# Four graph-attention layers: other all-node row tiles in layer 2, and other pools for the gathered rows

## The chip, the cores and the metric

The kernel runs on one core of a Trainium2 chip. The time is device time in microseconds, taken over several executions; beside it stands one execution recorded by the hardware profiler, with every instruction of the engines: PE (TensorE, matmuls; PEld are its weight loads), DVE (VectorE), ACT (ScalarE), POOL (GpSimd) and SP (SyncE, which issues most DMAs). Lower is better.

## The reference

There are 4096 nodes with 256 features and an adjacency matrix that has about 17 ones in a row of 4096 (each entry is one with probability 0.0039, and the diagonal is set). Four layers follow each other; each computes attention over the neighbours, adds it to its input and normalizes the row:

```python
# layers 0 and 1: 4 heads of 64; layer 2: 2 heads of 128; layer 3: 1 head, on x with both signs
e = leaky_relu(s1[:, None] + s2[None, :], 0.2)        # s1, s2: projections of x
att = softmax(where(adj > 0, e, -big), axis=1)
h = att @ Wh                                          # layer 3: also -softmax(-e) @ x, then fc_W and elu
x = layernorm(x + h)
```

Each layer needs the whole result of the layer before: a node's neighbours may lie anywhere.

## The kernel before

The 4096 rows are 32 row tiles of 128. The kernel keeps a table of projected rows in DRAM for each layer (the features times their exponentials, and the score terms), and works on a row tile in one of two ways.

A **sparse row tile** (class `RowTile`) collects only rows that its 128 nodes need. Lists made once from the adjacency (in layer 0, `lists`) name them. They are split in two parts. The *first part* (`half` 0) is the tile's own 128 rows, loaded by SP (line 808), and six indirect gathers of 128 rows each by GpSimd (line 813); these six read only rows of row tiles 0 to 22 (`MIX` is 23). The *second part* (`half` 1) is seven gathers that may read any row. So the first parts of a layer can be gathered once tiles 0 to 22 of the layer before are projected, and second parts only when all are. ACT then computes exponentials from the gathered score terms (line 923 in layers 0 to 2, 890 to 893 in layer 3), DVE masks them (925, 892, 894), and PE multiplies (946), 14 matmuls for a part and 28 instructions in the profile, since a float32 matmul is two.

An **all-node row tile** gathers nothing. `WHOLE` (line 115) lists, by layer, groups of up to four neighbouring row tiles that are computed densely against all 32 tiles of nodes: a pass of 32 units, each with one load of projected rows (`vw`, line 1206), the exponentials on ACT (1218; in layer 3, 1221 to 1225), the mask on DVE (1219, 1226) and matmuls for each tile of the group (1229). Layer 3 makes two passes over each group. The units are strewn between the parts of the sparse tiles by a budget (`whole`, line 1013), and all are used up some six parts before the layer's end. In layer 2, with 21 sparse and 11 all-node tiles, the passes are over 12-15, 28-31 and 25-27, in this order; the sparse tiles are 0-11 and 16-24.

**The end of a row tile.** `finish` and `norm` (lines 1395, 1339) divide, add, take the variance and scale. Several tiles share one inverse square root on DVE; `GROUPS` (line 82) says how many, by the layer and by the tile's number. Once scaled, a tile is *ready*; it is then projected for the next layer (class `Projection`: transpose on PE, copy `xT` on ACT, matmul at line 707, `row` on DVE, a store by SP at line 744), one or two per part, tiles below 23 first.

**The change of layer** (`close`, line 1124): the next layer's loads for its first row tiles are issued, ten all-node units of the next layer run ahead (`AHEAD`), the last tile is finished and projected, and the first parts of the next layer's tiles 0 and 1 are computed, in layer 3 not before the last projection.

**Slots.** Gathered rows stand in two pools of four slots, `g0` and `g1`. Up to layer 2 a part fills one slot; in layer 3, with longer rows, two. First parts use `g0`, second parts `g1`:

```python
    def slot(self, half, s):
        L, n = self.layer, self.layer.n
        if (half, s) not in self.slots:
            pool = L.prog.g1 if half else L.prog.g0
            self.slots[half, s] = pool.tile([P, SLOT], F32, name="G")
        return self.slots[half, s]
```

A slot is given out again in the order of the program; a gather or own-row load into it waits until the matmuls of its former owner are done. A planner orders the instructions of each engine before the program is built; each engine's queue, GpSimd's and SP's too, then runs strictly in that order, so that one waiting gather holds those behind it. In GpSimd's order, layer 2 begins with the first parts of tiles 0 to 3, one gather of tile 4's first part, the second parts of tiles 0 to 3, and the rest of tile 4; layer 3 begins with the first parts of tiles 0 and 1, then tile 2's and tile 3's mixed with the second parts of tiles 0 and 1.

Of the kernel before, what the change touches and what calls it, by code (L numbers as in the profile page):

```python
# [78 lines left out]
UNITS = (1 + FIRST, NPACK - FIRST)  # L79
FULL = ((0,), tuple(range(NPAIR - FIRST, NPACK - FIRST)))  # L80
PAIRS = (tuple(range(1, 1 + FIRST)), tuple(range(NPAIR - FIRST)))
GROUPS = (((24, 4),), ((24, 2), (29, 1), (31, 2)), ((16, 2), (17, 1), (20, 2), (25, 1), (31, 2)), ((25, 1), (28, 3), (31, 4)))
LEAD = 4
LATE = 4
MIX = 23
# [29 lines left out]
WHOLE = (  # L115
    (),
    (range(5, 8), range(29, 32),),
    (range(12, 16), range(28, 32), range(25, 28),),
    (range(28, 32), range(25, 28),),
)  # L120
AHEAD = 10
# [56 lines left out]
class Turns:  # L178
# [5 lines left out]
    def tile(self, *args, **kw):  # L184
        self.pools.append(self.pools.pop(0))
        return self.pools[-1].tile(*args, **kw)
# [586 lines left out]
class RowTile:  # L773
# [8 lines left out]
    def slot(self, half, s):  # L782
        L, n = self.layer, self.layer.n
        if (half, s) not in self.slots:
            pool = L.prog.g1 if half else L.prog.g0
            self.slots[half, s] = pool.tile([P, SLOT], F32, name="G")
        return self.slots[half, s]

# [8 lines left out]
    def load(self, half):  # L797
        L, m, n = self.layer, self.m, self.layer.n
        prog, nc, sh = L.prog, L.nc, L.shared
        copies = sh["v"][n]  # L800
        self.values = copies[m // BT % len(copies)]
        if half == 0:
            self.S = prog.ld.tile([P, H4, P], F32, name="S")
            nc.sync.dma_start(out=self.S[:, :TERMS[n]], in_=sh["e"][n][m].partition_broadcast(P))
            self.bits = prog.ld.tile([P, 2 * HALF, MW], I32, name="bits")
            if n > 0:
                nc.sync.dma_start(out=self.bits, in_=sh["bitsC"][m])
            nc.sync.dma_start(out=self.row(0, 0), in_=self.values[m * P:(m + 1) * P, :ROW[n]])
        else:
            self.y = L.load_x(m)  # L810
        for k in range(1 - half, HALF):
            pos = half * HALF + k - 1
            nc.gpsimd.indirect_dma_start(  # L813
                out=self.row(half, k), out_offset=None, in_=self.values[:N + 1 if half else MIX * P, :].rearrange("r (k c) -> (r k) c", k=STRIDE),
                in_offset=bass.IndirectOffsetOnAxis(ap=sh["idx"][:, m, pos:pos + 1], axis=0))
# [157 lines left out]
class Layer:  # L973
# [22 lines left out]
    def tile(self, m):  # L996
        if m not in self.tiles:
            self.tiles[m] = RowTile(self, m, self.order[m])
        return self.tiles[m]

    def load(self, m, half):
        if m < self.count and (m, half) not in self.loaded:
# [336 lines left out]
    def norm(self, y, m):  # L1339
# [8 lines left out]
        self.group.append((y, m))  # L1348
        if len(self.group) < next((size for end, size in GROUPS[self.n] if m < end), 1):
            return  # L1350
# [529 lines left out]
```

## Time and profile before

| | us |
|---|---|
| median of 3 runs (range) | 1991.31 (1989.16 to 1992.06) |
| profiled execution, its own time | 1986.33 |
| its span, first to last instruction | 1984.6 |
| PE busy | 1774.5 (89%) |
| PE weight loads busy | 1477.9 (74%) |
| ACT busy | 1560.2 (79%) |
| DVE busy | 1547.2 (78%) |
| GpSimd busy | 1386.2 (70%) |

The mean granted clock of PE is 0.939. Busy time is an average over stages with different limits; what bounds one stage is seen in windows of it. A row of a timeline gives the start, the length, the instruction and, in brackets, how long its engine was idle ahead of it and what ended that. A row of waits gives the sum, the number and the longest. DMA issue counts as idle time of the issuing engine: the 0.3 us ahead of each gather is such time. A releaser is inferred; where the one named had long been done, it was another.

### The profile page before, as it was taken

What the parts mean: (1) busy time and instruction counts of PE and PEld (TensorE: products, weight loads), DVE (VectorE), ACT (ScalarE), POOL (GpSimd) and SP (SyncE); (2) the same over time, 40 slices, a digit from 0 to 9 for tenths busy, and PEclk for the clock granted to TensorE, in tenths of its full rate; (3) what the DMA queues carried; (4) which work ended last, traced back from release to release, by engine and by line L of the source; (5) the groups of instructions that cost most, each with busy time, mean ns of one, the idle gap of its engine ahead of it and who ended that gap; (6) DMA issues with size and microseconds to landing.
All of it is one profiled execution on the core that took longest, in us unless ns stands there. A gap on an engine that the chain in (4) does not pass through costs nothing.

```text
span 1984.6 us, 47611 instructions
## 1 busy us (share of the span) xinstructions
PE 1774.5 (89%) x15397; PEld 1477.9 (74%) x15397; DVE 1547.2 (78%) x5213; ACT 1560.2 (79%) x4964; POOL 1386.2 (70%) x1387
## 2 busy tenths in 40 slices
PE   4758999999999889999999989799888999999894
PEld 3536777777777779989998779788776777777672
DVE  3457998888888788998998879688875577777765
ACT  4649989998879589999889879788783787777763
POOL 0057777777777777777777577777764777777773
PEclk8758899999999989999999999899999999999997
DMA  8799999999867767777777557677765888899883
GB/s 293 234 320 329 320 295 289 297 299 285 232 176 232 211 171 197 206 206 216 208 204 207 161 146 201 185 208 209 198 184 173 244 270 269 269 288 288 269 262 111
DMA packets 302523, 464.41 MB, mean 234 GB/s; under 512 B 91314, under 2 KB 216087, under 8 KB 302264
## 3 DMA queue, kind: packets, MB, share of 16 engines
q0 software_dynamic: 75296, 229.44, 39.9%
q1 hardware_dynamic: 222350, 227.63, 37.3%
q10 hardware_dynamic: 4618, 4.20, 0.6%
q8 instruction: 124, 2.03, 0.4%
q14 instruction: 135, 1.11, 0.2%
HBM read 412.03 MB, written 49.08 MB: 232 GB/s over the span
## 4 chain that ended last, share of the span: by engine, by line
PE 52%; DMA 13%; POOL 10%; ACT 9%; DVE 7%; issue 6%; SPq 1%; POOLq 0%; ACTq 0%; DVEq 0%
PE bank L946 25%; PE bank L1229 10%; POOL G L813 10%; DMA G<-vals,idx 7%; ACT w L923 5%; PE bank L707 5%; PE bank L1298 4%; PE bank L1296 3%; DMA raw<-in_adjB_dram 2%; DVE w L880 1%; ACT mk L415 1%; DMA vals<-row 1%; DMA G<-vals 1%; PE bank L693 1%; ACT pw L1218 1%
## 5 line engine op out<-in xcount | busy, mean ns | idle before, releaser
L813 POOL DMA_INDIRECT G<-vals,idx x1352 | 1380.9, 1021 | 568.4 <-issue 346.0
L923 ACT ACTIVATE w<-S,G 128x64 f32<-128x64 f32 (+1 forms) x3388 | 902.7, 350 | 103.7 <-DMA G<-vals,idx 88.9
L946 PE MATMUL bank<-G,w 128*64 128x130 f32 (+5 forms) x9044 | 903.7, 304 | 61.8 <-DVE w L880 51.5
L946 PEld LDWEIGHTS bank<-G,w 128*64 128x64 f32 (+1 forms) x9044 | 734.4, 156 | 208.6 <-DVE w L880 68.2
L1229 PE MATMUL bank<-vw,pw 128*128 128x129 f32 (+1 forms) x2304 | 378.5, 321 | 20.8 <-DVE pw L1219 6.0
L1229 PEld LDWEIGHTS bank<-vw,pw 128*128 128x128 f32 x2304 | 335.7, 194 | 59.1 <-issue 10.9
L880 DVE SCALAR_TENSOR_TENSOR w<-w,bank 128x1024 f32<-128x1024 f32 (+1 forms) x232 | 310.5, 1344 | 27.5 <-ACT w L923 26.5
L707 PE MATMUL bank<-wext,xT 128*128 128x268 f32 (+3 forms) x640 | 188.0, 429 | 27.6 <-ACT xT L698 26.0
L890 ACT ACTIVATE w<-S,G 128x64 f32<-128x64 f32 (+1 forms) x343 | 108.7, 352 | 75.6 <-DMA G<-vals,idx 59.9
L707 PEld LDWEIGHTS bank<-wext,xT 128*128 128x128 f32 x640 | 123.9, 210 | 51.7 <-ACT xT L698 29.2
L415 ACT ACTIVATE mk<-raw 128x1024 uint8<-128x1024 int32 x128 | 129.5, 1049 | 24.8 <-DMA raw<-in_adjB_dram 24.7
L1293 DVE SCALAR_TENSOR_TENSOR pw<-Sw,cw,mw 128x384 f32<-128x384 f32 x256 | 148.9, 609 | 0.1
L1298 PE MATMUL bank<-pw,vw 128*65 128x128 f32 x768 | 143.4, 274 | 0.0
L1219 DVE SCALAR_TENSOR_TENSOR pw<-pw,mw 128x512 f32<-128x512 f32 (+1 forms) x192 | 120.8, 642 | 28.6 <-ACT pw L1218 26.8
L1218 ACT ACTIVATE pw<-Sw,d 128x512 f32<-128x512 f32 (+1 forms) x192 | 126.3, 674 | 5.1 <-PE bank L1229 5.0
L1296 PE MATMUL bank<-vw,pw 128*128 128x65 f32 x768 | 128.0, 254 | 0.0
L1226 DVE TENSOR_TENSOR pw<-pw,mw 128x512 f32<-128x512 f32 (+1 forms) x128 | 79.0, 621 | 48.2 <-ACT pw L1223 23.4
L1296 PEld LDWEIGHTS bank<-vw,pw 128*128 128x128 f32 x768 | 113.8, 191 | 3.3 <-issue 0.7
L1221 ACT ACTIVATE pw<-Sw,d 128x512 f32<-128x512 f32 (+1 forms) x128 | 82.9, 655 | 15.6 <-PE bank L1229 5.6
L676 DVE TENSOR_TENSOR mw<-bw,pat 128x96 int32<-128x96 int32 (+1 forms) x352 | 89.0, 263 | 1.6
L698 ACT COPY xT<-bank 128x256 f32<-128x256 f32 x128 | 45.9, 360 | 48.7 <-PE bank L693 29.7
L892 DVE TENSOR_TENSOR w<-w,mk 128x512 f32<-128x512 f32 (+1 forms) x49 | 37.0, 756 | 53.7 <-ACT w L891 53.5
(197 smaller groups left out, 1908.4 us busy)
## 6 DMA issues: line engine op xcount, KB each, us to landing
raw<-in_adjB_dram SPq DMA_DIRECT2D x128, 512.0 KB
G<-vals,idx POOLq DMA_INDIRECT x1352
vw<-vals SPq DMA_DIRECT2D x128, 130.0 KB
vw<-vals SPq DMA_DIRECT2D x128, 128.5 KB
S<-edge SPq DMA_DIRECT2D x58, 256.0 KB
vw<-vals SPq DMA_DIRECT2D x96, 129.0 KB
xp<-y SPq DMA_DIRECT2D x96, 128.0 KB
y<-xp SPq DMA_DIRECT2D x96, 128.0 KB
```

The source lines that it names most:

```text
L415: nc.scalar.activation(self.mk[:, 2 * q:2 * q + 2], src, AF.Copy)
L707: nc.tensor.matmul(pp[:, :c1 - c0], self.xT[:, k, :], wext[:, k, c0:c1], start=(k == 0), stop=(k == KT - 1 and brow is None))
L813: nc.gpsimd.indirect_dma_start(out=self.row(half, k), out_offset=None, in_=self.values[:N + 1 if half else MIX * P, :].rearrange("r (k c) ...
L880: return nc.vector.scalar_tensor_tensor(pair, pair, LEAST, mh2, op0=ALU.max, op1=ALU.mult)
L923: nc.scalar.activation(w[h][:, u, rows], S[:, h, rows], AF.Exp, bias=d(g, h))
L946: nc.tensor.matmul(a, w[h][:, u, rows], b, start=half == 0 and u == 0 and (n == 3 or h == turns[0][0]), stop=half == 1, skip_group_check=True)
L1218: nc.scalar.activation(p, S[:, h, :g], AF.Exp, bias=d)
L1219: nc.vector.scalar_tensor_tensor(p, p, LEAST, mj, op0=ALU.max, op1=ALU.mult)
L1229: nc.tensor.matmul(accs[it][:, c:c + Wd], p[:, it, :], v[:, c:c + Wd], start=(j == 0 and h == heads[0]), stop=(j == NT - 1), skip_group_ch ...
L1293: nc.vector.scalar_tensor_tensor(p[h], S[:, h], c[:, j, h:h + 1], mj, op0=ALU.max, op1=ALU.mult)
L1296: nc.tensor.matmul(bu[:, it * Wd:(it + 1) * Wd], p[up][:, it, :], v[:, up * Wd:(up + 1) * Wd], start=j == 0 and it == 0, **how)
L1298: nc.tensor.matmul(bf[:Wd, it * P:(it + 1) * P], v[:, flat * Wd:(flat + 1) * Wd], p[flat][:, it, :], start=j == 0 and it == 0, **how)
```

## The change

Layer 2's row tiles 20 to 23 are all-node and 25 to 27 sparse, so that layer 2 has 20 sparse and 12 all-node tiles, in three passes of four: 12-15, 20-23, 28-31. The sparse ones are 0-11, 16-19 and 24-27. In `GROUPS`, layer 1's pairs reach up to tile 27 (24 to 28 were single before), and layer 2's grouping follows its new order. And the pools: in layer 2 the first parts of tiles 0 and 1 and all second parts use `g0`, and first parts from the third sparse tile on use `g1`; in layer 3 it is the other way round.

```diff
-GROUPS = (((24, 4),), ((24, 2), (29, 1), (31, 2)), ((16, 2), (17, 1), (20, 2), (25, 1), (31, 2)), ((25, 1), (28, 3), (31, 4)))
+GROUPS = (((24, 4),), ((28, 2), (29, 1), (31, 2)), ((24, 2), (28, 1), (31, 2)), ((25, 1), (28, 3), (31, 4)))
...
-    (range(12, 16), range(28, 32), range(25, 28),),
+    (range(12, 16), range(20, 24), range(28, 32),),
...
-            pool = L.prog.g1 if half else L.prog.g0
+            pool = L.pools(self.step, half)
...
+    def pools(self, m, half):
+
+        g0, g1 = self.prog.g0, self.prog.g1
+        if self.n < 2:
+            return g1 if half else g0
+        first, then = (g0, g1) if self.n == 2 else (g1, g0)
+        return then if half == 0 and m > 1 else first
```

In the changed program GpSimd's order at the start of layer 2 is: the first parts of tiles 0 to 5, then the second parts of tiles 0 to 5, and so on; at the start of layer 3: the first parts of tiles 0 to 3, then the second parts of tiles 0 to 3. The bits of row tiles 20 to 23 are also stored for all-node use (one store more in layer 0's list stage).

## The prediction

> **What bounds the kernel now.** I read the windows of the trace stage by stage first, then GpSimd's own timeline at the two layer changes, then the waits and PE's timeline. The stages: layer 1 runs at its even pace from 752 to 1095 us; layer 2's second parts begin to be gathered at 1134; layer 2's last gather is at 1477; layer 3's first sparse matmul is at 1528.5; PE ends at 1957. In the windows the columns are the stretch, its length, busy time (and instructions) of PE, PEld, DVE, ACT, POOL, then granted clock, DMA share, GB/s.
>
> ```profile
> 752.00:1095.00 343.00, 342.52 (x3732) 314.50 (x3731) 319.14 (x1002) 315.96 (x1226) 263.51 (x261) 1.00 0.73 207
> 1134.00:1181.00 47.00, 40.07 (x364) 37.84 (x362) 35.83 (x93) 35.34 (x93) 37.92 (x30) 1.00 0.52 141
> 1181.00:1478.00 297.00, 266.49 (x2304) 244.20 (x2305) 238.99 (x853) 234.48 (x719) 230.23 (x220) 0.96 0.72 199
> 1478.00:1528.00 50.00, 38.81 (x233) 30.54 (x232) 32.43 (x156) 21.78 (x58) 12.76 (x10) 0.90 0.48 142
> 1528.00:1568.00 40.00, 35.77 (x187) 26.93 (x185) 17.29 (x48) 24.58 (x51) 30.95 (x30) 1.00 0.84 247
> 1568.00:1716.00 148.00, 147.71 (x809) 114.18 (x810) 109.72 (x389) 116.31 (x264) 111.73 (x108) 0.99 0.86 265
> 1716.00:1800.00 84.00, 80.52 (x454) 59.03 (x453) 65.58 (x272) 62.20 (x152) 64.28 (x64) 0.98 0.90 285
> 1800.00:1900.00 100.00, 92.61 (x513) 68.84 (x513) 67.62 (x265) 72.50 (x179) 77.14 (x76) 0.97 0.88 275
> 1900.00:1957.00 57.00, 51.78 (x302) 35.89 (x298) 37.05 (x141) 37.98 (x95) 42.22 (x42) 0.97 0.80 241
> ```
>
> Layer 1 leaves PE 0.5 us idle in 343; layer 2, from 1134 to 1528, leaves it 6.9 + 30.5 + 11.2 = 48.6 us; layer 3 leaves 4.2 + 0.3 + 3.5 + 7.4 + 5.2 = 20.6 us. Why layer 2 idles is in GpSimd's timeline (start, length, and in brackets the idle time before) and in the waits from 1181 to 1528 (us, times, longest):
>
> ```profile
> 1119.48 1.38 POOL L813 DMA_INDIRECT G<-vals,idx  x1 [0.30 <-issue]
> 1134.24 4.06 POOL L813 DMA_INDIRECT G<-vals,idx  x1 [13.39 <-ACT w L923]
> 1477.23 1.03 POOL L813 DMA_INDIRECT G<-vals,idx  x1 [0.30 <-issue]
> 1512.80 1.23 POOL L813 DMA_INDIRECT G<-vals,idx  x1 [34.53 <-DMA y<-xp]
> ACT w L923 <- DMA G<-vals,idx: 55.9, 55, 2.9
> PE bank L707 <- ACT xT L698: 24.5, 11, 7.0
> PE bank L748 <- DVE row L741: 9.5, 9, 1.7
> ```
>
> GpSimd gathers without a pause from 1134 to 1478 and stands still for 13.4 us before and 34.5 us after. Its "busy" 78% is saturation: 0.30 us of issue precedes every gather of about 1 us. ACT waits for gathered rows 55 times; PE's waits for xT are the next link, since the copy stands behind those exponentials in ACT's queue. So layer 2 is bound by the gathers, with PE close behind at 90%.
>
> ```profile
> L813 POOL DMA_INDIRECT G<-vals,idx x261 | 263.5, 1010 | 79.6 <-issue 68.3 <-ACT w L923 4.3 <-DMA G<-vals,idx 2.4
> L813 POOL DMA_INDIRECT G<-vals,idx x220 | 231.1, 1050 | 67.1 <-issue 57.3 <-ACT w L923 2.7 <-PE bank L1229 1.5
> 1194.96 5.53 PE L1229 MATMUL bank<-vw,pw 128*128 128x129 f32 x48
> 1200.32 2.28 PE L946 MATMUL bank<-G,w 128*128 128x129 f32 x28
> 1206.23 2.73 PE L946 MATMUL bank<-G,w 128*128 128x129 f32 x28
> 1522.64 3.81 PE L707 MATMUL bank<-wext,xT 128*128 128x256 f32 x8 [7.03 <-ACT xT L698]
> ```
>
> These are the gather groups of layer 1's and layer 2's even stages, PE's pieces of layer 2, and the last projection, held 7 us. One gather of layer 2 costs (231.1 + 67.1) / 220 = 1.355 us.
>
> **The change, step by step.**
>
> *One sparse row tile becomes all-node.* GpSimd: 13 gathers fewer, 13 x 1.355 = 17.6 us. PE: two parts fewer, 2.28 + 2.73 = 5.0 us; the third all-node pass has four tiles instead of three, so 32 x 2 more matmuls, 128 instructions by 5.53 / 48 = 0.115, or 14.7 us. Net +9.7 us on PE. Durations of ACT and DVE are those of their groups by shape between 1134 and 1480. ACT: 28 exponentials fewer (20 by 0.285, 8 by 0.367 us, 8.6 us) and 64 wider by 0.704 - 0.578 (8.1 us): nothing. DVE: 64 wider by 0.679 - 0.539, 9.0 us, less the removed tile's masks, some 4, and less three of the inverse-root chains (the new groups make 74 of 77; 15 small instructions of 0.155, 7 us in layers 1 and 2): nothing. DVE and ACT at about 90% do not hold PE up, as layer 1's row shows (93% and 92% beside a full PE). SP: one more store of 256 KB in the list stage, at most 0.9 us at that stage's 290 GB/s, at least nothing; I take nothing, since 25 us of waits for raw loads are spread over that stage. Score rows and y loads balance.
>
> *The pools at the change to layer 2.* The 25th gather of layer 2 (1134.24) waited for a slot that row tile 0's first part held until its matmuls ended at 1133.5. In the changed program's order, first parts of tiles 4 and 5 stand ahead of all second parts and take slots that layer 1 let go by 1112. So 12 gathers, not one, fill the gap: 1120.9 + 12 x 1.3 = 1136.5. Tile 0's second part starts there, as before, but GpSimd is 11 gathers ahead (15 us). Layer 1's pairs (24, 25) and (26, 27) put one more projection into its closing: up to 3 us later, or 1 earlier; I take nothing, because GpSimd is occupied until 1136 anyway.
>
> *Layer 2's body.* Gathers left at 1136: 260 - 36 = 224, so the last is near 1136 + 304 = 1440, not 1477. PE's work is then the longer: from 1181 (until then both kernels wait for four contiguous second parts) 266.5 + 38.8 + 9.7 = 315 us, to 1496. Kept idle: the row-to-transpose waits, some 8 us. Layer 3's first sparse matmul comes at 1504 instead of 1528.5: **-24**.
>
> *The change to layer 3.* The 34.5 us wait is for row tile 22's projected rows: the first-part gathers read tiles 0 to 22, and 22 was the third last sparse tile. Now 20 to 23 are done in the second pass, and the last of them is 19, projected some 35 us of PE work before layer 3's first matmul: 10 us in four parts, 20 in eight projections, 5 in all-node units. Gathers can start near 1474. Tiles 0 and 1 take the slots of layer 2's first parts, 2 and 3 those of its second parts, so none waits for layer 3. All 24 are out near 1506, and the second parts follow when the last rows are written. Before, 10 were out at 1528.5. Lead gained: 14 gathers, 19 us, less 5: tile 1's second part now needs the slot of tile 1's first part, whose matmuls stand behind 52 all-node matmuls (11.5 us). On SP, the own-row loads of tiles 2 and 3 now wait for layer 2's last second parts, with four row stores behind them; bounded by 0 and the 2.7 us of a part, taken as nothing: the last projection comes later anyway.
>
> *Layer 3's body.* 1568 to 1716 is full and stays. Of the 20.6 us idle, a load of vw (3.0), the z copy between passes (5.3), a reciprocal (2.5) and vw again (2.1) are no gathers; the 8 left go, as the 14 us lead is larger: **-8**.
>
> *Clock.* The granted clock was 0.96 and 0.90 in layer 2's body and tail and 1.00 in the full stage. That is 297 x 0.04 + 50 x 0.10 = 17 us of clock lost, between none and most of it in working time; I take 4: **-4**.
>
> Sum: -24 - 8 - 4 = -36 us. The profiled execution took 1986.3; 1950 follows for its like. The median, 1991.3, lies 5.0 above it, so **1955** for the median.
>
> **Rules weighed.** The Trainium skill, "TensorE: Matmul & The Clock Gate", section on HAM oscillation, says gaps over about 3.4 us put PE to half clock for the next window. By that rule the 17 lost are 34 us at half speed and the gain could be 12 rather than 4; waits of 3.2 and 7.0 us in the tail fit it.
>
> A slowdown of the gathers by DVE is a rival of its own: if DVE's load, 80% in layer 2 and near 88% after, lengthened each of the 224 gathers by 0.16 us, the last would stay at 1476 and only layer 3's lead be left: 1991 - 4 = 1987. The rows speak against it (1.010 us beside DVE at 93%, 1.050 beside 80%). The Trainium skill, "SBUF — State Buffer", section on who interferes with whom, gives such a rule: GpSimd blocks while DVE holds the shared port.
>
> **The other rivals.**
>
> *PE does not pack.* If layer 2's idle is queue order and not gathers, 30.5 stay, 11.2 in the tail go, 9.7 are added, and 8 in layer 3 go: 1982. For it: the waits for gathers are short, 2.9 us at most. Against: layer 1, with the same order and full gathers, packs.
>
> *Slower.* The added 9.7 us of PE work are paid in layer 2's body, and its idle stays, because ACT or DVE takes the gathers' place; without a lead nothing goes in layer 3: 2001. It decides when less than 9.7 us of idle come back. For it: DVE rises to 88%. Against: layer 1's row.
>
> *Better.* All but the first 6.9 of layer 2's idle goes, most of layer 3's, and half the clock: 1936.
>
> *The pools do nothing* (slots were not what GpSimd waited for): then the 15 us lead is missing, the last gather is near 1458, still ahead of PE; 1960, inside the forecast's own range.
>
> **How the numbers follow.** Forecast 0.60 (1941 to 1969); better 0.10; PE does not pack 0.17 (1971 to 1990); slower gathers 0.05; slower 0.08. About 4 us (0.2%) is what a measurement can tell from no change. Faster: 0.60 + 0.10 + 0.14 + 0.02 = 0.86; same: 0.02 + 0.02 + 0.01 = 0.05; slower: 0.01 + 0.01 + 0.07 = 0.09. From 1936 to 1984 leaves out the slower cases and part of the unpacked one, some 0.18.
>
> **What would show it.** No GpSimd gap of 13 us near 1121, and 12 gathers in it; layer 2's body with PE idle under 4%; the wait of 34.5 us under 20 and not at the end; ACT waiting for gathers under 20 us in layer 2; first sparse matmul of layer 3 near 1504; PE's end near 1921. Wrong if ACT's waits for gathers stay, if GpSimd stalls over 10 us at tile 1's second part of layer 3, or if DVE becomes what PE waits for in layer 2.

## The result and the profile after

The changed kernel takes **1967.84 us** (median of 4 runs, 1963.39 to 1972.89; before, beside it, 1991.68): 0.9883 of before, 95% interval 0.9862 to 0.9904. A second set gave 1968.14 us, 0.9868 (0.9843 to 0.9894). The forecast was 1955, range 1936 to 1984. The medians lie 24 apart, where the sum had 36; the profiled execution took 1967.7 us, its span is 1965.8, 18.8 below before.

The windows of the changed kernel (stretch, length, busy time of PE, PEld, DVE, ACT, POOL, granted clock, DMA share, GB/s), layer 1's even stage first, then the beginning of layer 2's second parts, layer 2's body, the tail (the last projections), and layer 3's beginning in two stretches:

```profile
752.00:1095.00 343.00, 342.52 (x3740) 314.60 (x3738) 316.84 (x974) 316.25 (x1229) 264.28 (x259) 1.00 0.73 207
1134.00:1181.00 47.00, 44.58 (x401) 42.59 (x401) 36.35 (x93) 34.94 (x90) 36.93 (x34) 0.95 0.56 151
1181.00:1459.00 278.00, 264.68 (x2332) 246.36 (x2331) 237.09 (x809) 227.96 (x676) 219.30 (x193) 0.98 0.70 197
1459.00:1517.00 58.00, 45.22 (x272) 34.96 (x270) 37.74 (x190) 29.30 (x81) 24.94 (x25) 0.91 0.72 221
1517.00:1565.00 48.00, 47.78 (x255) 38.20 (x256) 29.48 (x94) 34.60 (x72) 25.32 (x24) 1.00 0.61 174
1565.00:1700.00 135.00, 135.00 (x754) 103.77 (x754) 98.38 (x355) 105.10 (x242) 102.20 (x99) 1.00 0.88 269
```

PE idles 13.3 us in layer 2's body (4.8%; before 30.5), but still 12.8 in the tail (before 11.2 of 50). GpSimd's timeline shows layer 2's last gather, the first of layer 3, and the first gathers of tile 0's and of tile 1's second part there:

```profile
1459.12 0.95 POOL L813 DMA_INDIRECT G<-vals,idx  x1 [0.30 <-issue]
1472.14 0.94 POOL L813 DMA_INDIRECT G<-vals,idx  x1 [12.07 <-PE bank L707]
1521.95 1.24 POOL L813 DMA_INDIRECT G<-vals,idx  x1 [17.75 <-DMA Sw<-edge]
1537.36 1.49 POOL L813 DMA_INDIRECT G<-vals,idx  x1 [6.49 <-ACT w L893]
```

The 13.4 us standstill at 1121 is gone and the 34.5 us one is 12.1. But the last gather of layer 2 is at 1459, not at 1440. The groups of gathers of layer 1's even stage and of layer 2, and ACT's wait for them from 1181 to 1520, say why:

```profile
L813 POOL DMA_INDIRECT G<-vals,idx x259 | 264.3, 1020 | 79.0 <-issue 68.0 <-ACT w L923 3.4 <-DMA G<-vals,idx 1.8
L813 POOL DMA_INDIRECT G<-vals,idx x194 | 220.9, 1139 | 59.1 <-issue 50.9 <-ACT w L923 2.4 <-PE bank L1237 1.8
```

```profile
ACT w L923 <- DMA G<-vals,idx: 28.0, 35, 3.2
```

A gather of layer 2 takes 1.139 us where it took 1.050: 194 x 0.089 = 17.3 us, nearly all of the 19 by which the last one is late. ACT waits for gathers 35 times, 28.0 us in all, instead of 55 times and 55.9.

### The profile page after: what moved, and what is told of

Read it like the earlier page. It is cut to its first block, busy times and chain, and to the rows that moved or that the text cites. A ratio compares the mean times of both kernels' runs of the same rounds, so it can differ in the third digit from the quotient of the medians.

```text
span 1965.8 us, 47661 instructions
## 1 busy us (share of the span) xinstructions
PE 1782.8 (91%) x15469; PEld 1490.5 (76%) x15469; DVE 1548.5 (79%) x5158; ACT 1558.2 (79%) x4936; POOL 1384.9 (70%) x1374
## 4 chain that ended last, share of the span: by engine, by line
PE 58%; DMA 11%; POOL 9%; ACT 8%; DVE 8%; issue 5%; SPq 1%; ACTq 0%; POOLq 0%; DVEq 0%
PE bank L946 27%; PE bank L1237 13%; POOL G L813 9%; DMA G<-vals,idx 6%; PE bank L707 5%; PE bank L1306 4%; ACT w L923 4%; PE bank L1304 3%; DMA raw<-in_adjB_dram 2%; DVE w L880 2%; ACT mk L415 1%; PE bank L693 1%; PE bank L538 1%; PE bank L540 1%; ACT pw L1226 1%
## 5 line engine op out<-in xcount | busy, mean ns | idle before, releaser
L1237 PE MATMUL bank<-vw,pw 128*128 128x129 f32 (+1 forms) x2432 | 390.8, 318 | 13.1 <-ACT zw L1400 5.3
L1237 PEld LDWEIGHTS bank<-vw,pw 128*128 128x128 f32 x2432 | 348.5, 193 | 51.0 <-issue 8.8
L707 PE MATMUL bank<-wext,xT 128*128 128x268 f32 (+3 forms) x640 | 183.1, 419 | 6.8 <-ACT xT L698 5.3
L1226 ACT ACTIVATE pw<-Sw,d 128x512 f32<-128x512 f32 x192 | 134.0, 711 | 11.7 <-PE bank L1237 11.1
L1227 DVE SCALAR_TENSOR_TENSOR pw<-pw,mw 128x512 f32<-128x512 f32 x192 | 129.2, 685 | 12.0 <-ACT pw L1226 10.9
L1304 PEld LDWEIGHTS bank<-vw,pw 128*128 128x128 f32 x768 | 113.8, 191 | 3.3 <-issue 0.5
L1229 ACT ACTIVATE pw<-Sw,d 128x512 f32<-128x512 f32 (+1 forms) x128 | 82.7, 655 | 18.4 <-PE bank L1237 9.9
L925 DVE SCALAR_TENSOR_TENSOR w<-w,mk 128x512 f32<-128x512 f32 (+1 forms) x80 | 59.6, 750 | 28.7 <-ACT w L923 28.6
```

Of the source, the lines that this page charges most:

```text
L707: nc.tensor.matmul(pp[:, :c1 - c0], self.xT[:, k, :], wext[:, k, c0:c1], start=(k == 0), stop=(k == KT - 1 and brow is None))
L1226: nc.scalar.activation(p, S[:, h, :g], AF.Exp, bias=d)
L1227: nc.vector.scalar_tensor_tensor(p, p, LEAST, mj, op0=ALU.max, op1=ALU.mult)
L1237: nc.tensor.matmul(accs[it][:, c:c + Wd], p[:, it, :], v[:, c:c + Wd], start=(j == 0 and h == heads[0]), stop=(j == NT - 1), skip_group_ch ...
L1304: nc.tensor.matmul(bu[:, it * Wd:(it + 1) * Wd], p[up][:, it, :], v[:, up * Wd:(up + 1) * Wd], start=j == 0 and it == 0, **how)
```

## The experiments

T0 is the first sparse matmul of layer 3. The tail goes from the transposes of the last projections (the two at once behind layer 2's body) to T0. The columns behind the ratio are of single profiled executions, in us; that of "pools only" took 1988.2, 6 above its median, that of before 1986.3, 5 below:

| kernel | median, ratio to before (95%) | tail starts | T0 | T0 to the end of the span | mean gather of layer 2 from 1181 | layer 2's last gather |
|---|---|---|---|---|---|---|
| before | | 1473.5 | 1528.5 | 456.1 | 1.050 | 1477.2 |
| changed | 1967.8, 0.9883 (0.9862 to 0.9904) | 1458.7 | 1517.3 | 448.5 | 1.140 | 1459.1 |
| changed, again | 1968.1, 0.9868 (0.9843 to 0.9894) | 1464.9 | 1520.5 | 447.5 | 1.146 | 1465.4 |
| tiles only | 1982.2, 0.9950 (0.9931 to 0.9969) | 1470.7 | 1526.4 | 456.3 | 1.112 | 1470.2 |
| pools only | 1982.2, 0.9953 (0.9933 to 0.9974) | 1469.4 | 1525.2 | 461.3 | 1.096 | 1472.1 |
| tiles and layer 2's pools | 1964.1, 0.9862 (0.9840 to 0.9884) | 1457.5 | 1509.7 | 452.9 | 1.105 | 1457.0 |
| exponentials behind | 1962.1, 0.9863 (0.9840 to 0.9887) | 1460.6 | 1516.2 | 444.2 | 1.129 | 1460.1 |

### The parts alone

The tiles and groups alone, with the pools as before:

```diff
-            pool = L.pools(self.step, half)
+            pool = L.prog.g1 if half else L.prog.g0
```

> Only the tile choice (and the groups that go with it); the pools stay as before. Theory (each part carries some of the gain, the pools by the 12 gathers that fill GpSimd's standstill before 1134): the 13 us standstill near 1121 is back, the last gather of layer 2 comes 10 to 13 us later than in the changed kernel (1469 to 1472 instead of 1459), and about half of the 24 us goes: 1978. Rival (the pools do nothing, the gain is the one sparse tile fewer): 1968, as the changed kernel.

Measured: 1982.24. The standstill is back, and longer (timeline):

```profile
1140.01 0.94 POOL L813 DMA_INDIRECT G<-vals,idx  x1 [19.44 <-issue]
```

The last gather is at 1470, 11 us behind that of the changed kernel's first execution and 5 behind that of its second; 10 to 13 were expected. The pools do something.

The pools alone, with tiles and groups as before (`WHOLE` and `GROUPS` put back):

> Only the pools; tiles and groups as before. Theory: no standstill near 1121, the last gather of layer 2 near 1466 instead of 1477, but the 34.5 us wait for row tile 22's rows stays and with it the late start of layer 3's gathers: 1981, 10 us below before. Rival 1 (pools do nothing): 1991. Rival 2 (pools are the whole gain): 1968.

Measured: 1982.17; no standstill at 1121, a wait of 35.5 us for layer 3's first gather. The theory holds in time; the last gather came at 1472, 6 later than expected.

Layer 2's pools with the tiles, without layer 3's:

```diff
-        if self.n < 2:
+        if self.n != 2:
             return g1 if half else g0
```

> The changed kernel with layer 3's slots as before; layer 2's new slots stay. Theory: the first sparse matmul of layer 3 stays at 1517, but GpSimd stands still once the first parts of tiles 0 and 1 have taken the first pool's four slots; the 8 us that layer 3's body gained are lost: 1976. Rival (gathers have slack in layer 3 anyway): 1968.

Measured: 1964.11. My theory falls: T0 comes 8 to 11 us earlier than in the changed kernel (1509.7), and the stretch behind it is 4 to 5 longer. The sum is the same within the intervals, as the rival had it. The order of PE's instructions is the same in both kernels up to the tail. So layer 3's rule buys little. With it PE idles 16.6 and 17.6 us between T0 and its last matmul in the changed kernel's two executions, without it 20.3; but the tail ahead of T0 is 58.6 and 55.6 us long with it, 52.2 without. The parts support each other: the tiles alone and the pools alone give 10.3 us each, the tiles and layer 2's pools together 28.4 (before took 1992.5 beside these runs). Layer 2's pools without the tiles were not run by themselves.

### What holds the tail

PE's longer waits in the tail of the changed kernel (timeline from 1459 to 1520), and ACT's own there (sum, times, longest):

```profile
1486.17 0.37 PE L748 MATMUL bank<-ident,row 128*1 128x128 f32 x1 [5.22 <-DVE b L1379]
1497.73 2.01 PE L707 MATMUL bank<-wext,xT 128*128 128x256 f32 x8 [1.07 <-ACT xT L698]
1503.65 0.27 PE L748 MATMUL bank<-ident,row 128*1 128x128 f32 x1 [3.91 <-DVE row L741]
1517.22 0.27 PE L748 MATMUL bank<-ident,row 128*1 128x128 f32 x1 [1.19 <-DVE row L741]
```

```profile
ACT w L890 <- DMA G<-vals,idx: 13.8, 8, 3.5
```

Line 890 is layer 3's exponentials of the first parts of tiles 0 and 1. They stand between the row exponentials and xT copies of the last projections, wait there for their gathers, and what stands behind them in ACT's queue is late. What the kernel holds back until the last projection are layer 3's matmuls on PE (T0 is at 1517.3, behind the transpose at 1517.22), not these exponentials. The trace of before has the same wait, only later: while PE waits 7.03 us for the last projection's xT (1515.6 to 1522.6), ACT's timeline reads:

```profile
1517.30 0.35 ACT L890 ACTIVATE w<-S,G 128x64 f32<-128x64 f32 x1 [2.78 <-DMA G<-vals,idx]
...
1521.37 0.35 ACT L890 ACTIVATE w<-S,G 128x64 f32<-128x64 f32 x1 [3.11 <-DMA G<-vals,idx]
...
1522.24 0.35 ACT L698 COPY xT<-bank 128x256 f32<-128x256 f32 x1
```

The edit keeps these exponentials, in the changed kernel, behind the last projection's edge copy on ACT (line 758, the copy of the score terms ahead of the last store):

```diff
-        nc.scalar.activation(erow[:T, k, :], self.pe[:T, :P], AF.Identity, bias=shift[:T, LOGS[n]:LOGS[n] + 1])
+        self.copied = nc.scalar.activation(erow[:T, k, :], self.pe[:T, :P], AF.Identity, bias=shift[:T, LOGS[n]:LOGS[n] + 1])
...
-                following.tile(0).half(0)
+                with self.prog.tc.issue_after(proj.copied.ins):
+                    following.tile(0).half(0)
                 for _ in range(AHEAD - 3):
                     following.unit()
-                following.tile(1).half(0)
+                with self.prog.tc.issue_after(proj.copied.ins):
+                    following.tile(1).half(0)
```

> The changed kernel, with the exponentials of layer 3's first two first parts queued on ACT behind the last projection's edge copy. Theory (in the tail these exponentials wait for gathers at the head of ACT's queue and hold the last projections back, 9 us of PE's 12.8 idle between 1459 and 1517): PE's idle in the tail falls to about 5 us, the last projection ends near 1508 instead of 1517, total 1960. Rival 1 (the tail is a chain of row, transpose and copy with its own latency): PE idles the same, 1968. Rival 2 (the exponentials then come too late and layer 3's first sparse matmuls wait): PE idles as much, but after the last projection, 1968 to 1972.

Measured: 1962.14. The waits of line 890 and PE's waits of 5.22 and 3.91 are gone; the transpose of the last projection's score terms comes at 1511.8, not 1508. PE idles 8.6 us in the tail, where 5 were expected (13.0 and 10.6 in the changed kernel's two executions), and the tail is hardly shorter (55.6 us), because a new wait takes their place: PE stands ready for layer 3's all-node units, whose score rows are not there (tiles 28 to 31, now layer 2's last pass).

```profile
1498.84 2.08 PE L1239 MATMUL bank<-vw,pw 128*128 128x257 f32 x4 [6.42 <-DVE pw L1236]
```

The time lies near the theory's, but its interval overlaps the changed kernel's, so a gain is not shown. The changed kernel was then measured a second time, as the measure for three more runs:

> The changed kernel once more, as the measure for the runs beside it on the same chip: 1968, 0.988 of before.

Measured: 1968.14, the second row of its name in the table. Beside it the same edit was tried with layer 3's old slots, and with these and layer 3's first all-node tiles 20 to 23 in place of 28 to 31:

```diff
-GROUPS = (..., ((25, 1), (28, 3), (31, 4)))
+GROUPS = (..., ((20, 1), (24, 4), (25, 1), (28, 3)))
...
-    (range(28, 32), range(25, 28),),
+    (range(20, 24), range(25, 28),),
```

> Layer 3's slots as before and the exponentials of its first two first parts behind the last projection's edge copy. Theory (what holds the last projections is these exponentials: with layer 3's new slots those of two tiles, with the old ones those of tile 0 alone, 4.7 us in one wait of PE at 1484): PE's 4.7 us wait is gone, 1959, 5 below the run with layer 2's slots alone (1964) and 9 below the changed kernel. Rival (the wait is replaced: PE's next work, the all-node units, then waits for the score rows of tiles 28 to 31, which come late, as the 6.4 us wait at 1498.8 in the run with the exponentials behind): 1963.

> As the run beside it (old slots of layer 3, exponentials behind), and layer 3's first all-node tiles are 20 to 23 instead of 28 to 31, so that their score rows are there when layer 2 ends; 28 to 31 become sparse in layer 3. Theory (after the exponentials, these score rows are the next wait of the tail, 6.4 us): 1953. Rival 1 (the rows were not the limit but the projections' own chain): 1959, as the run beside it. Rival 2 (other sparse tiles at layer 3's end cost more at the close): 1960 or more.

Measured: 1970.54 (0.9896, 0.9875 to 0.9917) and 1964.44 (0.9859, 0.9837 to 0.9881). In the second, PE's waits of the tail are down to these, and the tail is 48.5 us long with 3.6 idle, the shortest of all (the last line is its window):

```profile
1476.63 0.27 PE L748 MATMUL bank<-ident,row 128*1 128x128 f32 x1 [1.60 <-DVE u L1379]
1508.90 2.01 PE L707 MATMUL bank<-wext,xT 128*128 128x256 f32 x8 [0.85 <-ACT xT L698]
1512.01 0.27 PE L748 MATMUL bank<-ident,row 128*1 128x128 f32 x1 [1.11 <-DVE row L741]
1467.00:1516.00 49.00, 45.44 (x300) 36.67 (x297) 39.95 (x208) 23.95 (x70) 14.32 (x14) 1.00 0.65 200
```

Both forecasts of the time are misses all the same. The tail starts at 1464.9 and 1467.6, 7 and 10 us later than with layer 2's pools alone (1457.5), and the mean gather of layer 2 is 1.157 and 1.172 us. The function edited also closes layer 1, which I had overlooked: the edit moves layer 2's first exponentials too, and from there on the order of ACT and DVE differs. What the tail alone is worth cannot be read from these three runs. That these exponentials held PE, and behind them the score rows, is shown; that taking them away makes the kernel faster is not.

### Why the gathers are longer

One gather of the changed kernel took 5.32 us. GpSimd's timeline, and DVE's beside it:

```profile
1295.55 5.32 POOL L813 DMA_INDIRECT G<-vals,idx  x1 [0.30 <-issue]
1301.17 0.95 POOL L813 DMA_INDIRECT G<-vals,idx  x1 [0.30 <-issue]
1295.74 0.82 DVE L925 SCALAR_TENSOR_TENSOR w<-w,mk 128x640 f32<-128x640 f32 x1
1296.47 1.28 DVE L1227 SCALAR_TENSOR_TENSOR pw<-pw,mw 128x512 f32<-128x512 f32 x2
1297.68 0.20 DVE L676 TENSOR_TENSOR mk<-bits,pat 128x48 int32<-128x48 int32 x1
1297.80 0.68 DVE L1227 SCALAR_TENSOR_TENSOR pw<-pw,mw 128x512 f32<-128x512 f32 x1
1298.40 0.28 DVE L676 TENSOR_TENSOR mw<-bw,pat 128x128 int32<-128x128 int32 x1
1298.60 0.81 DVE L925 SCALAR_TENSOR_TENSOR w<-w,mk 128x640 f32<-128x640 f32 x1
1299.34 0.68 DVE L1227 SCALAR_TENSOR_TENSOR pw<-pw,mw 128x512 f32<-128x512 f32 x1
...
1300.64 0.16 DVE L1412 RECIPROCAL rec<-bank 128x2 f32<-128x2 f32 x1
```

While the gather lasts, DVE runs instructions that read two operands from SBUF, one behind the other, until a reciprocal that reads a PSUM bank. Of the 200 gathers that start between 1181 and 1481, the 103 that took under 0.965 us lie to 46% of their time beside such instructions, the 50 of 1.1 to 1.5 us to 83%. The Trainium skill, "SBUF — State Buffer", section "Who interferes with whom", has the rule: a DVE instruction with two SBUF inputs contends with a GpSimd instruction that reads SBUF. These shares agree with it, and the runs below put it to the test. First, layer 2's all-node units without mask and floor (left out of the computation), with one operand:

```diff
-nc.vector.scalar_tensor_tensor(p, p, LEAST, mj, op0=ALU.max, op1=ALU.mult)
+nc.vector.tensor_scalar(p, p, sh["shift2"], None, op0=ALU.max)
```

> The changed kernel, where layer 2's all-node units leave the mask and the floor out: DVE's instruction on the 128x512 tile has one operand from SBUF (a maximum with a constant column) instead of two; its count stays. DMA, ACT and GpSimd do the same work. Theory (GpSimd's gather waits while DVE strings instructions with two operands from SBUF: 83% of a gather of 1.1 to 1.5 us lies beside such instructions, 46% of one of 0.95): the mean gather of layer 2 between 1181 and the last one falls from 1.14 to about 1.00 us, none is over 2 us, and the last gather comes 20 us earlier, near 1440, as the prediction had it. Rival (long gathers come from the DMA queues or from the instruction's place in the program): 1.14 us, with several over 2 us, last gather near 1459.

Measured, in one execution: 1954.89 us. Groups of the gathers (1181 to 1446) and of the edited line:

```profile
L813 POOL DMA_INDIRECT G<-vals,idx x200 | 206.0, 1030 | 61.0 <-issue 50.0 <-ACT w L923 2.7 <-ACT pw L1226 2.1
L1227 DVE TENSOR_SCALAR pw<-pw,shift 128x512 f32<-128x512 f32 x151 | 77.9, 518 | 18.6 <-ACT pw L1226 17.7 <-issue 0.4
```

The last gather is at 1445, T0 at 1503.65, which is the forecast's 1504. But the instruction became shorter too (518 ns, not 685), and 48 of the 72 bit unpackings that the changed kernel has in this stretch had run before it, since nobody reads their masks any more. So DVE had less to do, and another rival, DVE's load, was not excluded. Two gathers were still over 2 us, where none was expected. So next, the whole computation, with the masks in free columns of the accumulation banks; first those of the all-node units, then those of the sparse parts as well:

```diff
-                    mj = self.bytes(bits, j)
+                    mj = self.bytes(bits, j, accs[j % g] if n == 2 else None)
...
+            mj = bank[:, BANK - g * P // 4:].bitcast(I32).rearrange("p (t i) -> p t i", t=g)
...
+            if n == 2:
+                there = accs[0][:, BANK - U * P // 4:].bitcast(I32).rearrange("p (t i) -> p t i", t=U)
```

> The changed kernel with the whole computation; in layer 2 the unpacked masks of the all-node units lie in the free columns of their accumulation banks instead of an SBUF buffer, so that DVE's mask instruction has one operand from SBUF. Theory (DVE's strings of instructions with two SBUF operands hold GpSimd's gathers up): the mean gather between 1181 and layer 2's last one falls from 1.14 to 1.05 us or below, the last is near 1446 instead of 1459 to 1465, total 1956. Rival (the run with the mask left out was faster because DVE had less to do, 221 us instead of 237, and not by the gathers): DVE does as much as in the changed kernel, total 1968. Second rival (DVE reading a bank that PE writes slows one of them): DVE's mask instruction takes more than 0.70 us instead of 0.685, total above 1968.

> As the run beside it, and the masks of layer 2's sparse parts lie in the free columns of their own accumulation bank too. Theory: mean gather near 1.02 us, last one near 1443, total 1953 to 1956 (PE is then what layer 2 waits for, so that little more comes of it). Rival: the unpacking now has to wait until the bank is free, DVE's queue stands behind it, and the total is above that of the run beside it.

Measured: 2053.03 (1.0309, 1.0282 to 1.0337) and 2061.93 (1.0354, 1.0329 to 1.0379): 85 and 94 us slower than the changed kernel. The waits of the first, from 1181 to 1500, show why (the first row was 5.8 us in the changed kernel from 1181 to 1459):

```profile
ACT pw L1226 <- PE bank L1237: 81.0, 79, 7.3
DVE bank L676 <- PE bank L1237: 27.7, 39, 1.4
DVE pw L1227 <- PE bank L1237: 26.5, 37, 1.5
PE bank L1237 <- DVE pw L1227: 24.9, 35, 1.5
```

By these rows the program waits for a bank as one thing: masks written and read there wait for the matmuls into the same bank, and the matmuls for them. DVE's own mask instruction kept its length (684 ns), so that the reason given by the second rival falls too, though the total is above 1968 as it said. For the time both theories missed. For the gathers the pair is the cleanest comparison of all: from 1300 to 1450 both kernels do the same work at the same pace, and differ in where the sparse mask lies. For the kernel with the all-node masks in banks, the window, then the groups of the gathers and of DVE's sparse mask instruction (`w<-w,mk`: the mask is in SBUF):

```profile
1300.00:1450.00 150.00, 138.05 (x1110) 119.66 (x1109) 118.52 (x387) 109.69 (x325) 97.73 (x97) 0.98 0.63 178
```

```profile
L813 POOL DMA_INDIRECT G<-vals,idx x97 | 97.7, 1008 | 52.4 <-issue 24.1 <-ACT w L923 22.3 <-ACT pw L1226 2.9
L925 DVE SCALAR_TENSOR_TENSOR w<-w,mk 128x640 f32<-128x640 f32 x16 | 13.2, 825 | 3.5 <-ACT w L923 3.5
```

The same of the kernel with both kinds in banks (`w<-w,bank`):

```profile
1300.00:1450.00 150.00, 138.69 (x1112) 119.46 (x1109) 117.94 (x392) 109.49 (x325) 95.02 (x100) 0.97 0.63 179
```

```profile
L813 POOL DMA_INDIRECT G<-vals,idx x100 | 95.0, 950 | 55.3 <-issue 26.2 <-ACT w L926 24.0 <-PE bank L1240 1.8
L928 DVE SCALAR_TENSOR_TENSOR w<-w,bank 128x640 f32<-128x640 f32 x17 | 13.6, 814 | 0.1
```

DVE is 79% busy in both, PE, ACT and DMA are alike. With the sparse masks in SBUF a gather takes 1.008 us and up to 1.59; with these in a bank too, 0.950 and none over 1.04. The whole stretch from 1181 to 1490 gives the same, 1.005 and 0.951. So it is the operands, not the load. A third run of this kind had both masks in banks and layer 3's old slots:

> As the run with both masks in banks, with layer 3's slots as before the change. Theory (of the two pool rules only layer 2's gains; layer 3's puts the exponentials of tile 1 among the last projections): 1950, 4 below the run with both masks. Rival (layer 3's slots make no difference): the same time.

Measured: 2069.37 (1.0400, 1.0374 to 1.0427). Beside a loss of 94 us it tells the two theories about the slots apart no better than before. Its gathers repeat the result: from 1300 to 1450 the mean is 0.949 us, and none is over 1.06.

Last, DVE was given more to do, with one operand:

```diff
+                            if h == heads[-1]:
+                                nc.vector.tensor_scalar(p[:, 0, :], p[:, 0, :], sh["shift2"], None, op0=ALU.max)
```

> The changed kernel with the whole computation and more work for DVE: in layer 2's all-node units, each second mask instruction is followed by a maximum with a column of -20 on 128x128 of its result, which changes no value and has one operand from SBUF (some 0.2 us, 74 of them between 1181 and 1459, 15 us). Theory (a gather is held up while DVE strings instructions with two SBUF operands, and gets through in the first one that has not): gathers over 2 us, 7 or 8 in the changed kernel, disappear; the time by which gathers over 1.5 us exceed 0.95 falls from 19 us to under 6, the last gather of layer 2 is near 1446 to 1450, total 1958. Rival (long gathers come from DVE's load as such): DVE's load rises from 85% to 90%, the mean gather stays at 1.14 or rises, total 1968 to 1975.

Measured: 1971.57 (0.9898, 0.9877 to 0.9918). Gathers from 1181 to 1468, and the window:

```profile
L813 POOL DMA_INDIRECT G<-vals,idx x199 | 227.5, 1143 | 60.7 <-issue 53.1 <-PE bank L1239 2.7 <-ACT w L923 2.1
```

```profile
1181.00:1468.00 287.00, 271.47 (x2399) 251.18 (x2399) 255.04 (x916) 234.18 (x696) 226.63 (x199) 0.99 0.67 193
```

My expectation failed: five gathers are over 2 us where seven were (the longest 3.57 instead of 5.32), and more are a little long, so the mean stays at 1.143. A pause of 0.289 us behind each second mask is not enough to shorten it. Mean and time lie where the rival, DVE's load, had put them (1.14 or more, 1968 to 1975), so this run does not speak for the operands; what does is the pair above. The run does show that 4 points more of DVE's load did not lengthen the mean. Share of the time in which DVE runs an instruction with two SBUF operands (from the timeline), and the mean gather in us (counted over whole windows, one gather more than in the first table):

| stretch | DVE busy | two SBUF operands | mean gather |
|---|---|---|---|
| before, layer 1 | 93% | 52% | 1.010 |
| before, layer 2 | 80% | 63% | 1.050 |
| changed, layer 2 | 85% | 68% | 1.139 |
| tiles and layer 2's pools | 87% | 70% | 1.107 |
| changed and pauses | 89% | 68% | 1.143 |
| one operand | 79% | 35% | 1.030 |
| all-node masks in banks | 79% | 34% | 1.008 |
| both masks in banks | 79% | 21% | 0.950 |

DVE's busy share does not order the gathers; the share with two operands does, but for two rows: layer 1 of before, and tiles with layer 2's pools. Nor does every such instruction count: the 21% that remain in the last row, most of them bit unpackings and additions, lengthen no gather beyond 1.04 us. Nor does the share give the size: from before to the changed kernel it rises by 5 points and the mean by 0.089, with the tiles and layer 2's pools by 7 points and 0.057. How a gather gets through between such instructions is open.

## Why the prediction was right and wrong

- **PE's added work**, +9.7: right. From 1134 to T0 PE is busy 354.6 us, before 345.8, which is 8.8 more.
- **The pools at layer 2's start**: right in place. Eleven gathers run in what was the gap (1121 to 1136; forecast 12), and tile 0's second part is no earlier (1138.9, before 1138.6). In size the rival "the pools do nothing" was wrong: without them the kernel takes 1982, not 1960. With longer gathers GpSimd bounds layer 2 again, and layer 2's pools are worth 18 us beside the tiles (1982.2 to 1964.1), no less than the 15 of their lead.
- **Layer 2's last gather at 1440**: this step failed. It took "224 gathers" by the 1.357 us of before's row. They took 0.089 us more, 17 us. In the one-operand run, with gathers of 1.030 us, T0 is 1503.65, the step's own 1504; but DVE had less to do there too. What hangs on the step was off as well: ACT's waits for gathers are 28.0 us and not under 20, PE's idle in the body 4.8% and not under 4, T0 1517.3 and not 1504, PE's end 1944.4 and not 1921. (Before's is 1962.0; the 1957 of the prediction is where its windows stop.) Slower gathers beside DVE stood among the rivals, at 0.16 us a gather and a chance of 0.05, but as a matter of DVE's load. I set it aside by layer 1's row (1.010 us beside DVE at 93%). That row speaks against the load and not against the operands: layer 1's sparse masks lie in a bank (`w<-w,bank`, line 880), layer 2's in SBUF (`w<-w,mk`, line 925).
- **The tail**: layer 3's gathers start at 1472 (forecast 1474), the 24 are out at 1503 (1506), tile 1's second part waits 6.5 us (5). But 12.8 us of PE's idle stayed in the tail, and 13.3 in the body, where the sum kept some 8 for both: this step failed too. The exponentials of layer 3 that come earlier wait in ACT's queue ahead of the last projections, and behind them PE waits for the score rows of tiles 28 to 31, which the change itself puts last. The forecast looked at GpSimd's and SP's queues there, not at ACT's, though it quotes the 7.03 us wait of before that has the same cause.
- **Layer 3's body**, -8: from T0 to the end it is 7.6 us shorter, but PE's idle up to its last matmul falls by 4.8 only (21.4 to 16.6). The lead of the new slots, the reason given, accounts for some 3 of these (20.3 with the old ones), and the total with the old ones is no worse. The size is in part luck.
- **The clock**, -4: clock lost in body and tail is 278 x 0.02 + 58 x 0.09 = 10.8 us instead of 17, but ahead of them 47 x 0.05 = 2.4 are lost where nothing was, and the mean of the whole execution stays 0.939. What it gave in time is not told apart. In the tail whose longest PE wait is 1.60 us (the window above) the granted clock is 1.00; in the tails of the table, each with a wait of 3.8 us or more, it is 0.86 to 0.94. Of the two waits that the prediction set beside the rule it takes from the Trainium skill, the one of 3.2 us is shorter than the 3.4 that it gives there, so that only the one of 7.0 fits.

The body and tail gave 11.2 us where 24 were forecast, the rest 7.6 of 12. The sign was right, and the time lies in the likeliest case, but by 1.2 us only, and with some luck. The steps gave 18.8 us of their 36. The forecast for the median had 5 us added because before's profiled execution lay that far below its median; the changed kernel's lies at its median, so this brought the forecast 5 us nearer by chance.

## What to carry to other kernels

Before a saving is counted as so many gathers by the length of one, look at what DVE will run beside them: in these runs mask instructions with two SBUF operands lengthened the gathers that GpSimd issues (1.14 us), those that read one operand or a bank did so much less (1.03, 0.95), and DVE's busy share hid the difference. Moving a mask into a bank that matmuls write cost far more here (85 us) than the gathers gave. When a stage's inputs come earlier, follow its consumers into the queues that they share with the stage before: here they came earlier too, and waited there in front of it. A rule that moves slots can pay in one layer and nothing in the next, so measure the halves apart.

## What was not expected of the hardware

The gather's length beside DVE's operands (0.95 to 1.17 us in the mean, 5.32 at the longest in the changed kernel) is the main one. DVE's mask instruction on 128x512 took 684 to 686 ns with its mask in a bank and 685 with it in SBUF, so that the place of an operand cost DVE nothing. And executions whose orders are the same up to the tail (the changed kernel twice, and tiles with layer 2's pools) reach it at 1457.5, 1458.7 and 1464.9: layer 2's body varies by 7 us, and the mean gather between 1.105 and 1.146. Why it varies is open.
